# Moving ScalarE's small work away from two slots, and one projection onto earlier slots, in a hand-ordered scan loop

## The chip, the cores and the metric

The kernel runs on one core of one Trainium2 chip. The metric is the device time of that core in microseconds (us). Four engines compute: TensorE (PE in the profile), VectorE (DVE), ScalarE (ACT) and GpSimd (POOL). A fifth queue, SyncE (SP), issues most DMAs. Each engine takes its instructions in the order in which the program wrote them, and waits for the others through semaphores.

## The reference

For an input x of 4 images, 512 channels, 64 x 64 positions (4096 tokens per image):

```
x = x + mamba_block(group_norm(x))      # layer 0
x = x + linear_attention(group_norm(x)) # layer 1
# layer 0, for each of 4 groups of 128 channels, with 256 inner channels:
xi, z = split(layer_norm(x) @ in_proj)
xc    = silu(causal_conv4(xi) + conv_b)
dt, B, C = split(xc @ x_proj);  dt = softplus(dt @ dt_proj + dt_b)
h_t = exp(dt_t * A) * h_{t-1} + (dt_t * xc_t) * B_t     # 16 states per inner channel
y_t = sum over states (h_t * C_t) + xc * D
out = (y * silu(z)) @ out_proj + skip * x
# then a layer norm and a 512 x 512 projection
# layer 1: q, k = relu(...), kq = sum over tokens of k q, out = (v kq / norm) @ w_out
```

All of it is in float32.

## The kernel before, in words

**Steps and slots.** The work is cut into 128 steps: 4 images x 8 tiles of 512 tokens x 4 groups of channels (`steps`, in this order). A step has 32 scans of 512 tokens, each over 128 partitions that hold 32 inner channels x 4 states; the loop takes them two at a time, so a step has `SLOTS` = 16 slots and the whole run 2048. In a slot stand, in the program's order:

- `drive(g+2)` on POOL (L655): the input of the scans (`bx`, 128 x 1024), two slots ahead; three buffers.
- two scans on DVE (L673), into `h`; after each, one `decay` on ACT (L647): the exponential `dA` (128 x 512, in PSUM), three scans ahead; three banks.
- between the two scans, `product` of the slot before on DVE (L696): three quarters of `h` times `c_all`, a bank of PSUM that `c_row` filled by a bf16 matmul. There is one such bank. `product` of an odd slot also issues `c_row` of the next pair of slots, and then `fold_states`: four fp32 matmuls that add the pair's states into `y`.
- in odd slots POOL multiplies the last quarter of `h` (L684).
- `after()`: everything else of the slot.

Two slots differ. `AWAY = (3, 10)` are the slots in which ACT changes its function table twice: in slot 3 to softplus and back (L1066, L1068), in slot 10 to silu and back. `BEHIND = (4, 11)` are the slots after them: there `product` of the slot itself comes right after its second scan, beside that of the slot before.

**What `after()` holds.** Work that is fixed to slots: the next step's time products `time_banks` at 2 and its softplus (`time_steps`) at 3; `out_proj` of the step before at 4 and its copy `with_skip` at 6; at 3, 5, 6, 7, 8 and 9 one piece of `front`, which is the generator `inputs` of the step after next; silu at 10. A matmul of 128 x 512 in fp32 counts as one unit in the program's own count (`work["mm"]`). The six pieces of `front` are: two taps of the convolution's first half (2 units), two more, the same for the second half, then the two products of the gate branch (`pz`, 1 unit each). A result is taken from PSUM by ACT one slot later, through `later(1, ...)`.

**Queues.** Then three queues of generators are asked for a piece each: `ahead` (the next tile's norms), `late` (the second layer norm and projection of the tile before) and `rest` (the attention of the image before). A piece of `late` or `rest` that needs TensorE is taken while `credit` lasts: 3.5 units a slot, less what the slot issued, and at most 2.6 saved. `limit` says how many of the three shared banks (`ps_w`) the queues may hold: 1 in slots 1 to 5, otherwise 2. A generator that yields "free" is asked again without credit. DVE's broad passes over 128 x 2048 (L390, L410) are "wide" and go into slots 3 and 10.

The order that results is fixed when the program is built.

Of the kernel before, what the change touches and what calls it, by code (L numbers as in the profile page):

```python
# [17 lines left out]
NTAP = 4  # L18
# [6 lines left out]
def kernel(  # L25
# [24 lines left out]
    nc = tc.nc  # L50
# [4 lines left out]
    NH = DI // P  # L55
# [21 lines left out]
    held, now, due = [0], [None], []  # L77

    def work_bank(name, behind=1):
        held[0] += behind  # L80
        return ps_w.tile([P, T], F32, tag="w", name=name)

    def free(n=1):
        held[0] -= n

    def later(n, what):

        done = []

        def both():  # L90
            what()
            done.append(True)

        if now[0] is None:
            both()
        else:
            due.append((now[0] + n, both))
        return done

    def soon():  # L100
# [3 lines left out]
    def until(*done):  # L104
        while not all(done):
            yield "wait"
# [4 lines left out]
    def room(when="wait"):  # L111

        while now[0] is not None and held[0] >= limit[0]:
            yield when

    limit, norming = [0], []
# [4 lines left out]
    def mm(out_, lhsT, rhs, abreast=1, **how):  # L121

        work["mm"] += (0.25 if rhs.dtype == BF16 else 1.0) * rhs.shape[-1] / T / abreast
        nc.tensor.matmul(out_, lhsT, rhs, **how)  # L124
# [188 lines left out]
    def aggregate(stats, name):  # L313

        mv = small.tile([P, NC, 2], F32, tag="mv", name=f"mv_{name}", bufs=4)
        for c in range(NC):
            nc.vector.bn_aggr(mv[:, c, :], stats[:, c, :, :].rearrange("p t s -> p (t s)"))
        return mv
# [37 lines left out]
    def bc(v, n):  # L356
        return v.unsqueeze(1).to_broadcast([P, n, v.shape[-1]])

    def layer_norm(v, name, gained):


        def means(parts, what, when):
            yield from room()
            sums = work_bank(f"{what}_sums_{name}")
            for c in range(NC):
                mm(
                    sums[c * LANE : (c + 1) * LANE, :], ones.to_broadcast([P, LANE]), parts[c],
                    start=True, stop=True, abreast=NC,
                )
            got = wk.tile([P, T], F32, tag="sq", name=f"{what}_got_{name}", bufs=4)  # L370

            def take():
                nc.scalar.copy(got, sums)
                free()

            copied = later(1, take)
            yield
            yield from until(copied)
            yield when
            yield from room(when)  # L380
            bank = work_bank(f"{what}_{name}")
            mm(bank, mean.to_broadcast([P, P]), got, start=True, stop=True)
            return bank

        while norming:
            yield "wait"
        norming.append(name)
        mu = yield from means([v[:, c, :] for c in range(NC)], "mu", "one ahead")
        yield "wide"
        nc.vector.tensor_tensor(v, v, bc(mu, NC), ALU.subtract)  # L390
        free()
        yield "free"
        sqs = []
        for c in range(NC):
            sqs.append(wk.tile([P, T], F32, tag="sq", name=f"sq_{name}_{c}", bufs=4))
            nc.scalar.activation(sqs[c], v[:, c, :], AF.Square)
            if c == 1:
                yield "free"
        var = yield from means(sqs, "var", "two ahead")
        rs = wk.tile([P, T], F32, tag="sq", name=f"rs_{name}", bufs=4)  # L400

        def root():
            nc.scalar.activation(rs, var, AF.Ln, bias=eps)
            nc.scalar.activation(var, rs, AF.Exp, scale=-0.5)

        rooted = later(1, root)
        yield
        yield from until(rooted)
        yield "wide"
        nc.vector.tensor_tensor(v, v, bc(var, NC), ALU.mult)  # L410
        free()
        norming.clear()
        yield
        if gained:
            for c in range(NC):
                nc.scalar.activation(
                    v[:, c, :], v[:, c, :], AF.Identity,
                    bias=b_sb[:, c : c + 1], scale=g_sb[:, c : c + 1],
                )
                if c % 2:  # L420
                    yield "free"
# [57 lines left out]
    def shifted(f, xt, t, nm):  # L479
        if t == 0:  # L480
            for o in range(NC):
                nc.vector.bn_stats(f["first"][:, o, 0, :], xt[:, o, :])
                if o % 2:
                    yield
            f["mv"] = aggregate(f["first"], f"first_{nm}")
            f["off"] = small.tile([P, NC], F32, tag="moff", name=f"moff_{nm}")
            nc.vector.tensor_scalar(f["off"], f["mv"][:, :, 0], -1.0, None, ALU.mult)
            nc.vector.memset(f["sum"][:, :, 0:1], 0.0)
            nc.vector.tensor_scalar(f["square"][:, :, 0], f["mv"][:, :, 1], float(T), None, ALU.mult)
            return  # L490
        for o in range(NC):
            for v, func in (("sum", AF.Identity), ("square", AF.Square)):
                unused = wk.tile([P, T], F32, tag="res", name=f"{v}_{nm}_{o}", bufs=2)
                nc.scalar.activation(
                    unused, xt[:, o, :], func, bias=f["off"][:, o : o + 1],
                    accum_out=f[v][:, o, t : t + 1],
                )
            yield "free"
# [13 lines left out]
    def inputs(f, xn, c, nm):  # L512

        xz = f["xz"] = wk.tile([P, 2, NH, T], F32, tag="xz", name=f"xz_{nm}", bufs=3)
        pc = [None] * NH

        def taps(e, ks):
            for k in ks:
                mm(
                    pc[e], w_cv[:, k, e * P : (e + 1) * P], xn[:, c, k : k + T],  # L520
                    start=(k == 0), stop=(k == NTAP - 1),
                )

        def take(e):
            nc.scalar.activation(xz[:, 0, e, :], pc[e], AF.Identity, bias=cb[:, e : e + 1])

        for e in range(NH):
            pc[e] = work_bank(f"pc_{nm}_{e}", 0)
            taps(e, range(NTAP // 2))
            yield  # L530
            taps(e, range(NTAP // 2, NTAP))
            later(1, lambda e=e: take(e))
            yield
        for e in range(NH):
            pz = work_bank(f"pz_{nm}_{e}", 0)
            mm(
                pz, w_z[:, e * P : (e + 1) * P], xn[:, c, NTAP - 1 : NTAP - 1 + T],
                start=True, stop=True,
            )

            later(1, lambda e=e, pz=pz: nc.scalar.copy(xz[:, 1, e, :], pz))
            yield

    def time_banks(f, nm):
# [62 lines left out]
    SLOTS = NH * NQ * JJ  # L607
    AWAY = (3, 10)
# [42 lines left out]
    def drive(g):  # L651
# [5 lines left out]
        )  # L657

    def slot(g, last, after):
        n, e, q, jj = place(g)  # L660
        b, t, c = steps[n]
# [68 lines left out]
    def with_skip(f, xn, c):  # L730
        nc.scalar.copy(xn[:, c, NTAP - 1 : NTAP - 1 + T], f["po"])
# [257 lines left out]
    ahead, late, rest, light = [], [], [], []  # L989

    def add_to(queue, pieces):
        queue.append([pieces, None])
# [40 lines left out]
    with tc.manual_schedule():  # L1033
        credit, seen, mix, held[0], held_x[0] = 0.0, work["mm"], iter(()), 0, 0
        for n, (b, t, c) in enumerate(steps):
            f, nm = fs[n], names[n]
            before = fs[n - 1] if n else None
# [8 lines left out]
            for s in range(SLOTS):  # L1046
                def after():
# [17 lines left out]
                    if s == 3 and nxt is not None:  # L1065
                        nc.scalar.preload_act_table_set("softplus")  # L1066
                        time_steps(nxt, names[n + 1])
                        nc.scalar.preload_act_table_set("natural_log_exp_and_others")  # L1068
                    if s == 6 and before is not None:
                        pb_, pt_, pc_ = steps[n - 1]  # L1070
                        with_skip(before, xn[pb_, pt_], pc_)
                        if pc_ == NC - 1:
                            add_to(late, leave(pb_, pt_))
                    if s in (3, 5, 6, 7, 8, 9):
                        next(front, None)
                    if s == 4 and nxt is not None:
                        to_rows(nxt, 0, names[n + 1])
# [1 line left out]
                    if s == 4 and before is not None:  # L1079
                        pb_, pt_, pc_ = steps[n - 1]  # L1080
# [16 lines left out]
                    ):  # L1097
                        one(light)

                    limit[0] = 1 if 0 < s < 6 else 2  # L1100
                    credit = min(credit + 3.5 - (work["mm"] - seen), 2.6)
                    busy = False
                    for queue in (ahead, late, rest):
                        kind = queue[0][1] if queue else None
                        if queue is ahead or kind == "free" or credit > 0 or kind == "more" and not busy:
                            start = work["mm"]
                            one(queue, ANYWHERE if queue is ahead and (c, s) > (1, 4) else may)
                            credit -= work["mm"] - start
                            busy = busy or work["mm"] - start > 1
# [68 lines left out]
```

## Time and profile before

| | |
|---|---|
| Time before, median of 3 | 8091.57 us (8079.1 to 8095.19) |
| The profiled execution: its own time | 8087.92 us |
| its span, first to last instruction | 8086.2 us |
| before the first scan | 120 us |
| the 2048 slots | 7492 us |
| after the last slot (attention of the last image) | 474 us |
| DVE busy | 7113.0 us (88%) |
| POOL busy | 6890.3 us (85%) |
| PE busy | 6471.4 us (80%) |
| ACT busy | 5514.5 us (68%) |
| TensorE clock granted, mean | 0.888 |

A share of the span is an average over everything; where the time of a slot goes is read from the idle time of DVE in that slot, and from what ended it. To say so by slot, the trace is cut at the start of each slot's first scan. The clock is the share of full speed that TensorE was granted.

### The profile page before, as it was taken

What the parts mean: (1) busy time and instruction counts of PE and PEld (TensorE: products, weight loads), DVE (VectorE), ACT (ScalarE), POOL (GpSimd) and SP (SyncE); (2) the same over time, 40 slices, a digit from 0 to 9 for tenths busy, and PEclk for the clock granted to TensorE, in tenths of its full rate; (3) what the DMA queues carried; (4) which work ended last, traced back from release to release, by engine and by line L of the source; (5) the groups of instructions that cost most, each with busy time, mean ns of one, the idle gap of its engine ahead of it and who ended that gap; (6) DMA issues with size and microseconds to landing.
All of it is one profiled execution on the core that took longest, in us unless ns stands there. A gap on an engine that the chain in (4) does not pass through costs nothing.

```text
span 8086.2 us, 92449 instructions
## 1 busy us (share of the span) xinstructions
PE 6471.4 (80%) x24800; PEld 2115.5 (26%) x24800; DVE 7113.0 (88%) x6815; ACT 5514.5 (68%) x8289; POOL 6890.3 (85%) x4597
## 2 busy tenths in 40 slices
PE   5677777667788878888788888888788888888599
PEld 1111111112222222322222222332222222322144
DVE  5999999999999999899999999999999999998600
ACT  4667777777767777677776767667777777776421
POOL 4999999999989989899998989888999999889600
PEclk8787888788899989898899999899889999999699
DMA  5666666666666666676666666667666666676402
GB/s 160 166 166 160 156 147 153 157 157 166 167 167 156 162 153 156 168 188 176 169 155 164 166 165 155 155 171 187 163 158 160 156 157 152 150 194 176 110 32 89
DMA packets 829199, 1265.98 MB, mean 157 GB/s; under 512 B 183912, under 2 KB 317560, under 8 KB 816384
## 3 DMA queue, kind: packets, MB, share of 16 engines
q1 hardware_dynamic: 804736, 1222.32, 59.7%
q0 software_dynamic: 16896, 33.56, 2.4%
q10 hardware_dynamic: 7040, 4.20, 0.2%
q8 instruction: 194, 3.18, 0.2%
q14 instruction: 333, 2.73, 0.1%
HBM read 1052.78 MB, written 206.57 MB: 156 GB/s over the span
## 4 chain that ended last, share of the span: by engine, by line
DVE 22%; PE 19%; DMA 17%; POOL 14%; issue 10%; ACT 9%; SPq 8%; POOLq 0%; DVEq 0%; ACTq 0%
DVE h L673 14%; POOL bx L655 10%; DMA d_all<-d_rows 9%; DVE h L696 7%; PE pq L124 5%; SPq L622 5%; DMA b_all<-b_rows 4%; ACT dA L647 3%; PE pc L124 3%; PE pr L124 3%; SPq L572 3%; PE y L124 3%; POOL h L684 2%; PE pp L124 1%; DMA c_sb<-c_rows 1%
## 5 line engine op out<-in xcount | busy, mean ns | idle before, releaser
L655 POOL TENSOR_TENSOR bx<-d_all,b_all 128x1024 f32<-128x1024 f32 x2048 | 4817.4, 2371 | 66.9 <-DVE h L673 51.5
L673 DVE TENSOR_TENSOR_SCAN h<-dA,st,bx 128x512 f32<-128x512 f32 x3584 | 4420.5, 1267 | 80.6 <-ACT dA L647 75.4
L647 ACT ACTIVATE dA<-d_all,a_t 128x512 f32<-128x512 f32 x4096 | 2780.4, 688 | 1764.2 <-DVE h L673 1727.5
L696 DVE TENSOR_TENSOR h<-h,c_all 128x768 f32<-128x768 f32 x2048 | 1906.7, 931 | 307.5 <-PE c_all L124 298.2
L124 PE MATMUL y<-h,fold 128*32 128x512 f32 x8192 | 1280.6, 701 | 160.5 <-POOL h L684 156.1
L684 POOL TENSOR_TENSOR h<-h,c_sb 128x512 f32<-128x512 f32 x1024 | 1299.3, 1269 | 121.4 <-DMA c_sb<-c_rows 33.5
L124 PE MATMUL pc<-xn,w_cv 128*128 128x512 f32 x2048 | 1078.8, 662 | 178.2 <-DVE xn L410 116.7
L124 PE MATMUL c_all<-parts,sel 128*128 128x384 bf16 x1024 | 368.3, 360 | 1058.5 <-DVE h L696 1056.1
L124 PE MATMUL pq<-w_qk,xa 128*128 128x512 f32 x2048 | 990.7, 615 | 1.9 <-ACT xa L348 1.9
L673 DVE TENSOR_TENSOR_SCAN h<-dA,bx 128x512 f32<-128x512 f32 x512 | 601.2, 1206 | 58.8 <-ACT dA L647 54.6
L124 PEld LDWEIGHTS pc<-xn,w_cv 128*128 128x128 f32 x2048 | 395.9, 204 | 807.7 <-issue 445.6
L124 PEld LDWEIGHTS <-sel 128*128 128x128 bf16 x1280 | 127.5, 100 | 1724.4 <-DVE h L696 1495.6
L683 POOL COPY st<-h 128x4 f32<-128x4 f32 x1024 | 206.9, 202 | 425.2 <-DVE h L673 382.2
L124 PEld LDWEIGHTS pq<-w_qk,xa 128*128 128x128 f32 x2048 | 402.8, 199 | 468.7 <-issue 446.2
L124 PE MATMUL pr<-xb,m 128*128 128x512 f32 x1024 | 500.4, 626 | 24.8 <-DMA xb<-x 16.5
L124 PE MATMUL pp<-xn,w_pr 128*128 128x512 f32 x1024 | 487.6, 602 | 3.8 <-DVE xn L410 3.8
L124 PEld LDWEIGHTS y<-h,fold 128*32 128x32 f32 x8192 | 170.9, 114 | 743.6 <-issue 281.0
L124 PE MATMUL y<-xz,dg 32*32 32x512 f32 x2048 | 340.4, 741 | 0.0
L720 POOL TENSOR_TENSOR xz<-xz 128x512 f32<-128x512 f32 x256 | 325.4, 1271 | 2.7 <-ACT xz L717 2.7
L561 POOL TENSOR_TENSOR dt<-dt,xz 128x1024 f32<-128x1024 f32 x128 | 302.2, 2361 | 25.5 <-ACT dt L553 25.5
L124 PE MATMUL pd<-xz,w_xp 128*128 128x512 f32 x512 | 311.6, 740 | 7.8 <-ACT xz L987 7.8
L771 ACT ACTIVATE kq<-pq 128x512 f32<-128x512 f32 x256 | 150.6, 588 | 232.6 <-PE pq L124 230.5
(169 smaller groups left out, 6063.9 us busy)
## 6 DMA issues: line engine op xcount, KB each, us to landing
d_all<-d_rows SPq DMA_DIRECT2D x2048, 256.0 KB, 6.6
b_all<-b_rows SPq DMA_DIRECT2D x4096, 64.0 KB, 2.2
d_rows<-dt SPq DMA_DIRECT2D x256, 512.0 KB, 3.7
c_sb<-c_rows SPq DMA_DIRECT2D x4096, 16.0 KB, 1.9
xs<-in_x_dram SPq DMA_DIRECT2D x32, 1024.0 KB, 5.8
xn<-in_x_dram SPq DMA_DIRECT2D x32, 1024.0 KB, 5.7
xr<-in_x_dram POOLq DMA_DIRECT2D x32, 1024.0 KB, 11.2
x<-xr SPq DMA_DIRECT2D x32, 1024.0 KB, 4.3
```

The lines of the kernel that those rows point to most:

```text
L124: nc.tensor.matmul(out_, lhsT, rhs, **how)
L561: nc.gpsimd.tensor_tensor(f["both"][:, 1], f["both"][:, 0], f["xz"][:, 0], ALU.mult)
L572: nc.sync.dma_start(d[k * BLK : (k + 1) * BLK, v], src)
L622: nc.sync.dma_start(dst[k * BLK : (k + 1) * BLK, :], rows_[q * KS + k, :].partition_broadcast(BLK))
L647: nc.scalar.activation(dAs[k], fs[n]["d_all", e][:, 0, j, :], AF.Exp, scale=a_t[:, e, j, q : q + 1])
L655: nc.gpsimd.tensor_tensor(bxs[g], fs[n]["d_all", e][:, 1, jj * 2 : jj * 2 + 2, :], bc(b_all[g // JJ], 2), ALU.mult)
L673: nc.vector.tensor_tensor_scan(h[:, j, :], dAs.pop(2 * g + i), bxs[g][:, i, :], 0.0 if t == 0 else st[:, c, e, q, j : j + 1], ALU.mult, AL ...
L683: nc.gpsimd.tensor_copy(st[:, c, e, q, :], h[:, :, T - 1])
L684: nc.gpsimd.tensor_tensor(h[:, :, CUT:], h[:, :, CUT:], bc(c_sb.pop(g // JJ), NJ), ALU.mult)
L696: nc.vector.tensor_tensor(own, own, bc(c_all[g // JJ], 2), ALU.mult)
L720: nc.gpsimd.tensor_tensor(f["xz"][:, 1, e, :], f["xz"][:, 1, e, :], f["xz"][:, 0, e, :], ALU.mult)
L771: nc.scalar.activation(qk[i], pq, AF.Relu)
```

## The change

1. `later`: what falls due in slot 3 or 10 is done in the slot after.
2. In those two slots a piece of `late` or `rest` that yielded "free" (work of ACT, mostly) is not taken. Two `yield`s of those generators now say "free": in `layer_norm` before the gain, and in `shifted` ahead of its eight ACT passes.
3. `front` has four pieces instead of six, at slots 5, 6, 7 and 8: the two products of the gate branch stand beside the two pieces of the convolution's first half (3, 3, 2 and 2 units).
4. `with_skip` (and the start of `leave`) moves from slot 6 to slot 5.
5. `limit` is 0 in slot 3, 1 in slots 1, 2, 4, 5 and 6, otherwise 2.

```diff
-            due.append((now[0] + n, both))
+            at = now[0] + n
+            due.append((at + 1 if at % SLOTS in AWAY else at, both))
...
         norming.clear()
-        yield
+        yield "free"
         if gained:
...
             return
+        yield "free"
         for o in range(NC):
             for v, func in (("sum", AF.Identity), ("square", AF.Square)):
...
-        for e in range(NH):
-            pc[e] = work_bank(f"pc_{nm}_{e}", 0)
-            taps(e, range(NTAP // 2))
-            yield
-            taps(e, range(NTAP // 2, NTAP))
-            later(1, lambda e=e: take(e))
-            yield
-        for e in range(NH):
+        def gate_branch(e):
             pz = work_bank(f"pz_{nm}_{e}", 0)
             mm(
                 pz, w_z[:, e * P : (e + 1) * P], xn[:, c, NTAP - 1 : NTAP - 1 + T],
                 start=True, stop=True,
             )
-
-            later(1, lambda e=e, pz=pz: nc.scalar.copy(xz[:, 1, e, :], pz))
+            later(1, lambda: nc.scalar.copy(xz[:, 1, e, :], pz))
+
+        for e in range(NH):
+            pc[e] = work_bank(f"pc_{nm}_{e}", 0)
+            taps(e, range(NTAP // 2))
+            if e == 0:
+                gate_branch(0)
+            yield
+            taps(e, range(NTAP // 2, NTAP))
+            later(1, lambda e=e: take(e))
+            if e == 0:
+                gate_branch(1)
             yield
...
-                    if s == 6 and before is not None:
+                    if s == 5 and before is not None:
...
-                    if s in (3, 5, 6, 7, 8, 9):
+                    if s in (5, 6, 7, 8):
                         next(front, None)
...
-                    limit[0] = 1 if 0 < s < 6 else 2
+                    limit[0] = 0 if s == 3 else 1 if s in (1, 2, 4, 5, 6) else 2
...
                         kind = queue[0][1] if queue else None
+                        if kind == "free" and s in AWAY and queue is not ahead:
+                            continue
```

## The prediction

> **What bounds the kernel now.** First the page: no engine is full, DVE comes nearest.
>
> ```profile
> PE 6471.4 (80%) x24800; PEld 2115.5 (26%) x24800; DVE 7113.0 (88%) x6815; ACT 5514.5 (68%) x8289; POOL 6890.3 (85%) x4597
> ...
> L673 DVE TENSOR_TENSOR_SCAN h<-dA,st,bx 128x512 f32<-128x512 f32 x3584 | 4420.5, 1267 | 80.6 <-ACT dA L647 75.4
> ...
> L696 DVE TENSOR_TENSOR h<-h,c_all 128x768 f32<-128x768 f32 x2048 | 1906.7, 931 | 307.5 <-PE c_all L124 298.2
> ```
>
> The last column is DVE's idle time ahead of the group. Where nothing waits, a slot lasts 3.22 us (two scans, one product). The step's mean is 58.6 us over the 126 middle steps; DVE idles 3.48 of them (438 us in all). By slot: 1.71 in slot 4, 0.50 in slot 12, 0.47 in slot 7, 0.28 in slot 5, under 0.17 elsewhere. So the question is who ends DVE's waits in these four slots. The waits of DVE, longest first:
>
> ```profile
> DVE h L696 <- PE c_all L124: 298.2, 165, 6.0
> DVE kq L778 <- PE pk L124: 242.4, 42, 7.6
> DVE h L673 <- ACT dA L647: 130.1, 64, 46.7
> ```
>
> The second is the attention of the last image, after the slots, and is not touched. The first is 207 us in slot 4 and 52 in slot 7; the third is 62 in slot 12, 18 in slot 5, and start-up. A timeline of slots 3 and 4 of step 90 shows how slot 4 comes to wait (start, length, engine, line):
>
> ```profile
> 5382.49 2.08 PE L124 MATMUL pt<-dt,w_dt 32*128 32x512 f32 x4
> 5385.96 3.78 PE L124 MATMUL pc<-xn,w_cv 128*128 128x512 f32 x4 [1.39 <-DVE xn L410]
> 5389.53 2.57 PE L124 MATMUL pr<-xb,m 128*128 128x512 f32 x4
> 5391.94 0.33 PE L124 MATMUL c_all<-parts,sel 128*128 128x384 bf16 x1
> ```
>
> and DVE at the same time:
>
> ```profile
> 5387.86 1.27 DVE L673 TENSOR_TENSOR_SCAN h<-dA,st,bx 128x512 f32<-128x512 f32 x1
> 5392.30 0.95 DVE L696 TENSOR_TENSOR h<-h,c_all 128x768 f32<-128x768 f32 x1 [3.17 <-PE c_all L124]
> ```
>
> In slot 4 the row of C is asked for one scan (1.2 us) before its use, and it stands behind slot 3's work: a piece of the convolution that waited for a bank (here until DVE's wide pass had read it), then `pr`. And the four `pc` matmuls took 3.78 us, against 2.57 for four of `pr` half of which ran at full speed. The windows of this step say why (last but two: clock):
>
> ```profile
> 5377.20:5380.40 3.20, 1.40 (x10) 0.25 (x9) 3.20 (x4) 2.42 (x5) 2.96 (x4) 1.00 0.90 191
> 5380.40:5385.80 5.40, 4.17 (x16) 0.70 (x12) 5.40 (x5) 3.40 (x5) 5.32 (x4) 0.53 1.05 212
> 5385.80:5393.20 7.40, 7.24 (x19) 2.64 (x19) 4.23 (x6) 3.90 (x5) 7.37 (x4) 0.65 0.69 166
> 5393.20:5395.50 2.30, 2.30 (x15) 0.82 (x12) 2.30 (x3) 0.69 (x1) 0.00 (x0) 1.00 0.47 179
> ```
>
> PE was quiet in slot 2 (1.40 us busy), and ran slots 3 and 4 at 0.53 and 0.65 of its clock. Over all steps the clock is 0.76, 0.76, 0.79, 0.83 in slots 1 to 4 and 0.97 to 0.99 in 5 to 9.
>
> **What the Trainium skill says, and whether this trace agrees.** (1) The Trainium skill, *TensorE: Matmul & The Clock Gate*, section "Part 1: The HAM clock gate": after one idle window of about 3.4 us TensorE runs at half clock, and about one busy window brings it back. The trace agrees: its clock records are 0.5 or 1.0 and multiples of 3.413 us long. Of 167 such windows at full clock with PE under 40% busy none was followed by a fast one; of those over 50% nearly all; of 261 half-clock windows over 90% busy, 88%. (2) The same page, section "Step-by-step: what each phase is for": matmuls stay in program order. Agrees: `c_all` ran after `pr`. (3) *ScalarE: Activation LUTs*, section "What ACT_TABLE_LOAD costs": 1283 ns, plus a drain of 1380. The trace has 1283 ns and the next activation 0.02 us later: no drain, and I use 1.28.
>
> **The change, part by part** (per step; 126 steps count).
>
> *Slot 4.* In the changed program's order the work that PE gets in slot 3's `after()` falls from 3.0 to 0.3 units. Nothing then stands ahead of the row of C. 1.68 us (what this product waits) become about 0.1: **-1.58**.
>
> *Slots 5 to 7.* The 2.7 units go to slots 5 and 6. Between the row for slot 4 and the row for slot 6 PE now has 9.35 units instead of 7.89 (quarter points 8, 9.5, 11; before 6, 8, 9.25). Time there: from the end of slot 4's first product to the product of slot 7 are 8.9 us without waits, so that row must start 8.4 us after the first one. In before, a full-clock stretch with 10 units took 9.4 us: 0.36 for the row and about 0.88 a unit. For 7, 8, 9.5 and 11 units (shares 0.2, 0.2, 0.25, 0.35) that is 6.5, 7.4, 8.7 and 10.0 us: late by 0, 0, 0.3 and 1.6, mean 0.64. At half clock more. After slot 2's work (about 3.5 us) PE has nothing until the row of slot 4: 3 us where slot 3 has no wide pass, over 5 where it has (2.26 us more, 67 of 126 steps). That makes an idle window in my estimate in 85% of the steps. The burst then starts at half clock and stays there for the rest of that window and one full one, 3.4 to 6.8 us, mean 4.8: 2.4 us of work lost. Late then by 0.5, 1.4, 2.7, 4.0, mean 2.46. 0.85 x 2.46 + 0.15 x 0.64 = 2.19, against 0.41 now: **+1.78**. The next row (slot 9's product) has 6.7 units instead of 6.1 and PE no lead: 8 units in a quarter of the steps are 1 us late: 0.38 against 0.09, **+0.29**.
>
> *ACT at the table changes.* In slot 12 DVE waits for `dA` in the 40 steps whose slot 10 has no DVE extra, 1.47 us each. Two loads, silu (1.91) and a `dA` (0.69) are 5.2 us behind the one before; the DVE work in that time leaves 0.7 us. The gate's copy (0.58) and the `shifted` passes (0.14 of each kind, about 0.9 a pair) account for the rest, and leave: 40 x 0.77 and small ones, **-34 us** over the run. Slot 5's 18 us go to a third: **-12**. The order shows slot 3 not free of other work: the next tile's `group_norm` (L348, half an activation a step) stays.
>
> *Where it goes.* The moved copies stand in slots 4 to 9. ACT idles 16.4 us a step, and a `dA` is 2 us early there or more; nothing on DVE waits. `with_skip`, a slot earlier, may wait for `po` on ACT with two `dA` behind it; those have the same lead. POOL's instructions and SP's DMAs keep their slots (a store of the attention may go one later). POOL is 2.7 to 6 us ahead of the scans in slots 5 to 8, so it does not become the bound for a gain of 1.6. The tail holds 475.1 units either way. A little more attention falls into slots 13 to 1: **+8**.
>
> Sum: 126 x (1.78 + 0.29 - 1.58) = +62; -34 - 12 + 8 = -38; **+24 us** on the profiled execution's 8087.9, so **8112 us**. The median shown stands 3.7 above that execution, inside the spread of 16.
>
> **The rivals.** *A, the forecast:* the wait moves from slot 4 to slot 7 and grows, since PE goes cold in the emptied slot 3. *B, on the other side:* PE stays warm. With share p of cold starts the sum is 126 x (0.64 + 1.82 p - 0.41 + 0.29 - 1.58) - 38; at p = 0 that makes 7916, at 0.5 8031; it turns at 0.75. For it: slot 3's own stalls on banks are gone, and PE that was cold in slot 2 works longer and may be warm by then. Against: the counts above. *C:* the two cancel, within 0.2%. *D:* A, and PE's lateness reaches ACT, which waits in order for `po`, `pz`, `pc` and `y` in slots 5 to 9 with the `dA` behind: 0.6 us more a step, 8190. Against: ACT waits 1.0 us a step for these now (xz L717 99.9 us, xz L525 22.2, the others 4.4), and it shows nowhere on DVE. *E, the edit does less than it says:* `group_norm` in slot 3 keeps some of slot 5's wait; worth at most 12 us.
>
> **How the numbers follow.** 0.2% (16 us) is about what a measurement of this kernel can tell from no change. A 0.44 and D 0.12 are slower: 0.56; C 0.12; B 0.32. The predicted time is A's, 8112, whose own range is 8100 to 8170. B reaches down to 7916, and lies at 8031 where half of the steps are warm; I take 7985 below and D's 8190 above.
>
> **What would show it.** Right: DVE's wait for `c_all` nearly gone in slot 4 and 2 us in slot 7; clock at slots 4 and 5 below 0.8; slot 12's wait for `dA` halved. Wrong: clock over 0.85 in slots 4 to 5 and slot 7's wait under 1 us (B), or `dA` waits on DVE in slots 6 to 10 (D).

## The result, and the profile after

The changed kernel is slower: 8215.80 us (median of 4 runs, 8211.47 to 8218.85) against 8089.92 (8079.10 to 8095.19), a ratio of 1.0158 [1.0145, 1.0171]. Its profiled execution took 8218.36 us (span 8216.4), 130 us more than that of the kernel before. The forecast, 8112, had the side right and the size wrong; its range ended at 8190.

The page of the changed kernel, busy time and costliest groups (last column: idle time of the engine just before the group, and what ended most of it):

```profile
PE 6489.0 (79%) x24800; PEld 2118.6 (26%) x24800; DVE 7121.6 (87%) x6815; ACT 5516.5 (67%) x8289; POOL 6886.4 (84%) x4597
...
L678 DVE TENSOR_TENSOR_SCAN h<-dA,st,bx 128x512 f32<-128x512 f32 x3584 | 4433.2, 1271 | 109.1 <-ACT dA L652 54.4
...
L701 DVE TENSOR_TENSOR h<-h,c_all 128x768 f32<-128x768 f32 x2048 | 1916.2, 936 | 383.6 <-PE c_all L125 365.5
```

DVE is busy for only 8.6 us more than before, so nearly all of the loss is waiting. The waits of DVE, us in total, times, longest:

```profile
DVE h L701 <- PE c_all L125: 365.5, 179, 8.6
DVE kq L783 <- PE pk L125: 251.4, 46, 7.6
DVE h L678 <- ACT dA L652: 109.7, 71, 48.5
DVE h L678 <- POOL bx L660: 56.1, 45, 5.7
```

The wait for `c_all` grew by 67 us and that for `dA` fell by 20. The last line was 6.8 us before: here is a wait that the prediction said would not come. "The row" of a slot is, in what follows, the bank `c_all` that its product reads; one row serves two slots, so the rows that matter are those for slots 4, 6 and 8, and a late one shows as a wait in slot 4, 7 or 9. Cut by slot over the 126 middle steps (DVE's idle time, us):

| | before | after | change | forecast |
|---|---|---|---|---|
| `c_all`, slot 4 | 208 | 3 | -205 | -199 |
| `c_all`, slot 7 | 52 | 258 | +206 | +224 |
| `c_all`, slot 9 | 11 | 45 | +34 | +37 |
| `dA`, slots 12 and 5 | 81 | 56 | -25 | -46 |
| `bx` of POOL | 6 | 55 | +49 | 0 |
| `c_all`, slot 15 | 18 | 52 | +34 | } +8 |
| attention and statistics | 40 | 59 | +20 | |
| other `c_all` and `dA`; gaps under 150 ns | 23 | 32 | +9 | 0 |
| all of DVE's idle time | 438 | 561 | +123 | +24 |

With the 8 us by which DVE is busier in these steps, that is the whole 130. The attention after the last slot takes the same time in both (474 and 473 us). The first three rows come to +35 against a forecast of +62; the loss that was missed is below them.

First the part that was right. PE in slots 4 to 7 of step 90 of the changed kernel (start, length, line, operation; the last bracket is the idle time before):

```profile
5481.70 0.50 PE L125 MATMUL c_all<-parts,sel 128*128 128x384 bf16 x1 [3.66 <-DVE h L701]
5482.13 1.94 PE L125 MATMUL y<-h,fold 128*32 128x512 f32 x8
5484.00 1.93 PE L125 MATMUL po<-xn,skd 32*32 32x512 f32 x8
5485.86 2.47 PE L125 MATMUL po<-xz,w_op 128*128 128x512 f32 x4
5488.17 1.88 PE L125 MATMUL pp<-xn,w_pr 128*128 128x512 f32 x4
5489.89 1.88 PE L125 MATMUL pc<-xn,w_cv 128*128 128x512 f32 x4
5491.60 1.02 PE L125 MATMUL pz<-xn,w_z 128*128 128x512 f32 x2
5492.46 1.88 PE L125 MATMUL pp<-xn,w_pr 128*128 128x512 f32 x4
5494.18 0.33 PE L125 MATMUL c_all<-parts,sel 128*128 128x384 bf16 x1
5494.43 1.07 PE L125 MATMUL y<-h,fold 128*32 128x512 f32 x8
```

DVE, at the product that needs the second row:

```profile
5488.20 2.45 DVE L678 TENSOR_TENSOR_SCAN h<-dA,st,bx 128x512 f32<-128x512 f32 x2
5494.54 0.95 DVE L701 TENSOR_TENSOR h<-h,c_all 128x768 f32<-128x768 f32 x1 [3.89 <-PE c_all L125]
```

The row for slot 4 now leaves as soon as DVE has freed its bank: nothing stands ahead of it, and PE had been idle for 3.66 us. Then slot 4's own work (`y`, `po`) and the moved work come in one block of 12 us without a gap, and the row for slot 6 stands behind it. Its first half runs slowly: the eight `y` matmuls take 1.94 us at the block's start and 1.07 at its end. The windows of slots 2 to 6 of this step (after the length: busy time of PE, PEld, DVE, ACT and POOL; then PE's clock, the DMA share and GB/s):

```profile
5470.90:5474.10 3.20, 1.03 (x5) 0.29 (x9) 3.20 (x4) 2.42 (x5) 2.96 (x4) 0.86 1.06 212
5474.10:5479.50 5.40, 3.94 (x20) 0.50 (x12) 5.40 (x5) 3.39 (x5) 5.32 (x4) 0.77 1.07 214
5479.50:5483.80 4.30, 2.10 (x9) 0.31 (x9) 4.20 (x5) 3.90 (x5) 4.30 (x3) 0.56 0.57 150
5483.80:5486.20 2.40, 2.40 (x13) 0.54 (x10) 2.40 (x4) 0.69 (x1) 2.40 (x2) 0.50 0.42 114
5486.20:5489.40 3.20, 3.20 (x7) 1.30 (x7) 3.20 (x5) 1.72 (x3) 3.12 (x4) 0.90 0.72 285
```

The clock is 0.56 and 0.50 in slots 4 and 5; in the kernel before the cold slots of this step were 3 and 4. Over all steps the clock in slots 4 and 5 is 0.70 and 0.70 (before 0.83 and 0.99), and 76% of the steps have over 1 us at half clock between the two rows. The forecast had 85%.

### The profile page after: what moved, and what is told of

Same layout as the page of the kernel before. It is cut to its first block, busy times and chain, and to the rows that moved or that the text cites. A ratio compares the mean times of both kernels' runs of the same rounds, so it can differ in the third digit from the quotient of the medians.

```text
span 8216.4 us, 92462 instructions
## 1 busy us (share of the span) xinstructions
PE 6489.0 (79%) x24800; PEld 2118.6 (26%) x24800; DVE 7121.6 (87%) x6815; ACT 5516.5 (67%) x8289; POOL 6886.4 (84%) x4597
## 4 chain that ended last, share of the span: by engine, by line
PE 23%; DVE 21%; DMA 18%; POOL 12%; issue 10%; SPq 8%; ACT 6%; POOLq 0%; DVEq 0%; ACTq 0%
DVE h L678 13%; DMA d_all<-d_rows 10%; POOL bx L660 8%; DVE h L701 6%; PE pq L125 4%; SPq L627 4%; PE y L125 4%; PE pc L125 3%; PE po L125 3%; DMA b_all<-b_rows 3%; SPq L577 3%; ACT dA L652 3%; PE pr L125 2%; POOL h L689 2%; PE pp L125 2%
## 5 line engine op out<-in xcount | busy, mean ns | idle before, releaser
L125 PE MATMUL y<-h,fold 128*32 128x512 f32 x8192 | 1334.4, 729 | 194.9 <-POOL h L689 190.0
L125 PE MATMUL pc<-xn,w_cv 128*128 128x512 f32 x2048 | 1014.0, 618 | 5.3 <-ACT xn L417 4.6
L125 PEld LDWEIGHTS pc<-xn,w_cv 128*128 128x128 f32 x2048 | 369.4, 192 | 615.7 <-issue 580.8
L125 PE MATMUL po<-xz,w_op 128*128 128x512 f32 x512 | 293.6, 700 | 2.0 <-POOL xz L725 2.0
```

## The experiments

Unless said otherwise the diff is against the changed kernel, and the ratio against the kernel before on the same chip (8086.8 to 8088.0 us).

### Which part costs

`act_only`: parts 1 and 2 alone; the changed kernel without the new `front`, `with_skip` and `limit`.

```diff
-                    if s == 5 and before is not None:
+                    if s == 6 and before is not None:
...
-                    if s in (5, 6, 7, 8):
+                    if s in (3, 5, 6, 7, 8, 9):
...
-                    limit[0] = 0 if s == 3 else 1 if s in (1, 2, 4, 5, 6) else 2
+                    limit[0] = 1 if 0 < s < 6 else 2
```

> Parts 1 and 2 of the change alone, on the kernel before (what falls due in slots 3 and 10 a slot later, 'free' pieces not taken there); the gate's second copy stays in slot 10, since silu needs it. Theory A (the loss is TensorE's: its work is crowded into slots 4 to 6 after an empty slot 3): these parts are no loss; DVE's wait for dA in slot 12 falls from 62 us to 30 to 45, nothing else moves: 8050 to 8085 against 8090. Rival R1 (ACT's moved work is late where it went, in slots 4 to 9, and holds back POOL and DVE): a large part of the +126 us shows here: 8130 or more.

`pe_side`: parts 3, 4 and 5 alone.

```diff
-            due.append((at + 1 if at % SLOTS in AWAY else at, both))
+            due.append((now[0] + n, both))
...
-        yield "free"
+        yield
...
-                        if kind == "free" and s in AWAY and queue is not ahead:
-                            continue
```

> Parts 3, 4 and 5 alone (four front pieces at slots 5 to 8, with_skip at 5, the limits), without parts 1 and 2. A: the whole loss is here, 8210 to 8250; DVE waits about 2 us a step for c_all in slot 7, at a clock of 0.7 in slots 4 and 5. R1: less than half of it, under 8150.

`act_only` took 8071.73 us, 0.9980 [0.9973, 0.9987]; `pe_side` 8240.56, 1.0189 [1.0172, 1.0206]. What relieves ACT gains 15 us (slot 12's wait for `dA` falls from 62 to 51, less than the 30 to 45 expected); what moves PE's work costs 154, more than the whole change, as A expected. The waits of DVE in `pe_side`:

```profile
DVE h L699 <- PE c_all L124: 377.3, 188, 11.4
...
DVE h L676 <- POOL bx L658: 45.3, 43, 5.4
```

The `c_all` waits come with parts 3 to 5, and so do most of those for POOL. But `act_only` has some of these too, 20 us where the kernel before had 7:

```profile
DVE h L675 <- POOL bx L657: 20.1, 33, 2.3
```

### Cold clock or too much work between the two rows

The forecast let both act: 9.35 units instead of 7.89, and half clock. `after_warm` keeps PE busy in slot 3 with matmuls by a zero operand: six, and more after a wide pass.

```diff
+                    if s == 3:
+                        for _ in range(6 + round(3.5 * extra[0])):
+                            nc.tensor.matmul(
+                                ys[n, 0], minus[0 : 2 * LANE, :], bqk[0 : 2 * LANE, :],
+                                start=False, stop=False, skip_group_check=True,
+                            )
```

> The changed kernel, with matmuls of zeros added to y at the end of slot 3 (64 rows of bf16 zeros, 512 columns; 6 of them, and 3.5 for each us of DVE's additional work in that slot), which change no value and wait for nothing: TensorE does not stand idle in slot 3. A1 (of the 2.05 us wait in slot 7 most is half clock): clock in slots 4 and 5 rises from 0.70 to 0.9 or more, slot 7's wait falls to 0.6 to 1.0 us, 8215 to 8040 - 8090. A2 (it is the 9.35 units of work, or banks, at whatever clock): the wait stays over 1.6 us and the time is 8180 or more; the zeros themselves may even delay the row of slot 4.

8184.12 us, 1.0121 [1.0106, 1.0136]: a miss for A1; A2 had the time and the delayed row, but not the wait. Slots 4 and 5 have a clock of 0.84 and 0.83, and slot 7's wait falls only from 258 to 177 us (1.4 a step, where A2 expected over 1.6); and the zeros stood ahead of the row of slot 4, whose wait is 85 us again.

`after_thin45` takes work out instead: no queue piece that needs a bank in slots 4 and 5.

```diff
-                    limit[0] = 0 if s == 3 else 1 if s in (1, 2, 4, 5, 6) else 2
+                    limit[0] = 0 if s in (3, 4, 5) else 1 if s in (1, 2, 6) else 2
```

> The changed kernel with limit 0 in slots 4 and 5 as well: the queues open no bank there, so TensorE has 7.0 units (in every step) between the rows for slots 4 and 6, not 9.35, and 8.5 instead of 6.7 between the rows for slots 6 and 8. A1 (half clock costs 2.4 us in most steps): slot 7 still waits 0.4 to 0.8 us and slot 9 about 1: 8100 to 8150. A2 (work alone): with 7 units nothing waits in slot 7, slot 9 0.3 us: about 8000.

8146.53 us, 1.0071 [1.0055, 1.0086], inside the range of A1; its waits were split otherwise. Slot 7's falls to 40 us (0.31 a step, expected 0.4 to 0.8) with the clock at 0.72 and 0.70, but the work comes back ahead of slot 9, whose wait rises from 45 to 185 (1.5 a step, expected 1).

`after_front3` starts `front` in slot 3 again, in pieces of 2, 3, 3 and 2 units.

```diff
-            if e == 0:
-                gate_branch(0)
+            if e == 1:
+                gate_branch(1)
...
             if e == 0:
-                gate_branch(1)
+                gate_branch(0)
...
-                    if s in (5, 6, 7, 8):
+                    if s in (3, 5, 6, 7):
```

> The changed kernel with the first front piece (2 units) back in slot 3 and the gate's products one piece later: pieces of 2, 3, 3 and 2 units at slots 3, 5, 6 and 7. Between the rows for slots 4 and 6 TensorE still has 9.2 units (9.35 in the changed kernel), but slot 3 is not empty. A1 (half clock): clock in slots 4 and 5 over 0.85, slot 7's wait falls from 2.05 us to under 1.0, slot 4's comes back to 0.4 to 0.9: 8110 to 8170. A2 (only the number of units counts): slot 7 still waits 1.8 us or more, and slot 4 0.5: 8230 or more.

8193.66 us, 1.0132 [1.0116, 1.0149], outside what either theory expected. The clock is back at 0.80 and 0.97, yet slot 7 still waits 155 us, and slot 4 waits 131 again. The means (9.2 units, 1.2 us a step) hide two kinds of steps. In 39 of the 126 PE still has over 1 us at half clock between the two rows, and these hold 95 of the 155 us. At full clock 7 or 8 units wait 0.03 us a step (53 steps), and about 11 units 2.0 (25 steps): what does not fit at full clock is the steps with most work.

`after_front3_thin` is the opposite case: pieces of 2, 3, 2 and 3 at slots 5 to 8, no queue piece with a bank in 3, 4 and 5, so that 6.0 units lie between the rows and PE stays cold.

```diff
-            if e == 0:
-                gate_branch(0)
...
-            if e == 0:
-                gate_branch(1)
+            gate_branch(e)
...
+                    limit[0] = 0 if s in (3, 4, 5) else 1 if s in (1, 2, 6, 7) else 2
```

> As after_2332_gap, but limit 0 in slots 3, 4 and 5 and 1 in slots 1, 2, 6 and 7: 6.0 units between the rows for slots 4 and 6 in every step, and 8.5 before the next. A: slot 7 waits under 0.1 us although the clock in slots 4 and 5 is 0.7, slot 9 1.0 to 1.4 us: 8040 to 8100. Rival (the cold clock alone brings slot 7's wait, whatever the work): slot 7 waits over 0.5 us.

8086.98 us, 1.0002 [0.9993, 1.0010]. The clock is 0.71 and 0.68, as cold as in the changed kernel, and slot 7's waits for `c_all` are 2.3 us in all. **A cold start alone makes no wait: 6 units fit even so.** The queue work returns before slot 9 (177 us). All of DVE's waits for `c_all`:

```profile
DVE h L698 <- PE c_all L125: 226.9, 142, 5.1
```

The changed kernel itself shows the two together. Its steps sorted by units between the rows, with slot 7's mean wait: 7 units, 0.60 us where PE had over 1 us at half clock (14 steps) and none otherwise (6); 8 units, 1.37 us at low clock (19) and 0.08 at full clock (10); 9 to 10.2 units, 1.85 (11) and 0.24 (8); above, 3.64 (52) and 1.79 (6). So at full clock up to 9 units nearly fit, and at half clock even 7 are late.

### Other places for the work

`after_front6789`: `front` one slot later, and no bank for the queues in 3, 6 and 7; some of the attention is then left for after the slots, where the time grows from 474 to 488 us.

```diff
-                    if s in (5, 6, 7, 8):
+                    if s in (6, 7, 8, 9):
...
+                    limit[0] = 0 if s in (3, 6, 7) else 1 if s in (1, 2, 4, 5) else 2
```

> The changed kernel with the four front pieces at slots 6, 7, 8 and 9, and limit 0 in slots 3, 6 and 7, otherwise 1 in slots 1 to 5; the convolution's second result is taken in slot 10 ahead of silu. Slot 3 is as empty as in the changed kernel, but between the rows for slots 4 and 6 stand 6.5 units, then 7.1, then 8.0. The attention is not finished in the slots: 32 units more come after them, about +28 us. Theory A: half clock in slots 4 and 5 as before (0.7), yet slot 7 waits under 0.4 us, since 6.5 units cold fit the 8.4 us; slots 9 and 11 wait 0.3 to 0.6 each: 8050 to 8110 with the tail. Rival (what counts is that slot 3 is empty, wherever the work goes): 8200 or more.

8079.73 us, 0.9990 [0.9984, 0.9997], in the range of theory A: slot 7's wait is 54 us (0.43 a step, where under 0.4 was expected), with slot 3 still empty and the clock at 0.68 and 0.71 in slots 4 and 5. What is new is 70 us in slot 11.

`act_lim3`: `act_only`, with no bank for the queues in slot 3 (`limit[0] = 0 if s == 3 else 1 if 0 < s < 6 else 2`).

> Parts 1 and 2 (as in act_only) and of part 5 limit 0 in slot 3 alone; the front pieces and with_skip stay where the kernel before has them. TensorE's work from slot 3 falls from 3.0 to 2.0 units and does not become empty. Theory A (an emptied slot 3 and a crowd in slots 4 to 6 are the loss; less in slot 3 is good): DVE's wait for c_all in slot 4 falls from 1.66 us to about 0.8 (steps of the kernel before with 2 units there waited 0.46), slot 7's rises by 0.1 to 0.3: 7960 to 8040. Rival (what leaves slot 3 only comes back as a wait in slot 7): 8060 or more.

8062.09 us, 0.9964 [0.9951, 0.9977]: the rival's side, at its edge. Slot 4's wait falls from 209 to 130 us only: the first piece of the convolution is still in slot 3. Of the 79 us gained there 58 come back as waits in slots 7 and 9 (against `act_only`).

`after_2332_gap`: pieces of 2, 3, 2 and 3 at 5 to 8, and no bank for the queues in 3, 4 and 6.

```diff
+            gate_branch(e)
...
+                    limit[0] = 0 if s in (3, 4, 6) else 1 if s in (1, 2, 5, 7) else 2
```

> The changed kernel with the same four slots for front, but each gate product beside a second half (pieces of 2, 3, 2 and 3 units at slots 5 to 8), and limit 0 in slots 3, 4 and 6, 1 in slots 1, 2, 5 and 7. Between the rows of C for slots 4 and 6 stand 7.2 units (at most 8.25; the changed kernel 9.35, up to 11.25), then 7.4 and 6.3; the attention is finished in the slots. Theory A (a cold start of 2.4 us in three steps of four, and 0.88 us a unit): slot 4 waits 0, slot 7 0.4 to 0.6 us, slot 9 0.3 to 0.6; with bx, slot 15 and attention as in the changed kernel 7990 to 8060, ahead of both. Rival (the wait only moves on, to slot 9 or 11): 8100 or more.

8066.56 us, 0.9976 [0.9966, 0.9987]; a little above the expected range. Slot 7 waits 58 us, as expected, and slot 9 83 (0.66 a step, expected 0.3 to 0.6).

`spread_3678`: one piece early, three late, and a gap for the queues ahead of slot 9's row.

```diff
+            gate_branch(e)
...
-                    if s in (5, 6, 7, 8):
+                    if s in (3, 6, 7, 8):
...
-                    limit[0] = 0 if s == 3 else 1 if s in (1, 2, 4, 5, 6) else 2
+                    limit[0] = 0 if s in (3, 7) else 1 if s in (1, 2, 4, 5, 6) else 2
```

> The changed kernel with front pieces of 2, 3, 2 and 3 units at slots 3, 6, 7 and 8 (each gate product beside a second half) and limit 0 in slots 3 and 7. Slot 3 keeps 2 units, so TensorE is not empty there; 5.9, 6.1, 6.4 and 6.9 units stand before the rows of C for slots 4, 6, 8 and 10 (in the changed kernel 3.9, 9.4, 6.7 and 5.2). Theory A (what a row waits for is the units between it and the last row, plus half clock after a quiet slot): DVE waits 100 to 140 us for c_all in slot 4 as in the other kernels with 2 units in slot 3, under 30 us each in slots 7, 9 and 11; clock in slot 5 over 0.95; bx near 20: 7985 to 8030, the fastest of all. Rival (each move only sends the wait on): 8060 or more.

**8030.08 us, 0.9926 [0.9913, 0.9940]: faster than both kernels**, at the upper end of what was expected. Its clock in slots 4 and 5 is 0.80 and 0.97. Slot 4 keeps 139 us, slot 7 has 13, slot 9 35, slot 11 28; `bx` is 33, where 20 was expected. Its waits of DVE:

```profile
DVE h L698 <- PE c_all L125: 253.0, 197, 6.1
...
DVE h L675 <- ACT dA L649: 80.8, 38, 46.0
DVE h L675 <- POOL bx L657: 33.2, 34, 3.7
```

Against the changed kernel 112 us of `c_all` and 29 of `dA` are gone, and 23 of `bx`.

### Why POOL became late

In the changed kernel the `bx` waits lie in slots 8 (38 us) and 7 (11). Two edits move work of POOL. `after_pad` takes away a wait of POOL, for the norm that it copies from (34 us of POOL's idle time in slot 7):

```diff
         yield from layer_norm(body, f"a_{b}_{t}", True)
+        yield from pause(1)
         nc.gpsimd.tensor_copy(pad, xn[:, :, T : T + NTAP - 1])
```

> The changed kernel with the copy of the tile's last columns on POOL (pad, once in four steps) one slot later. In the changed kernel POOL waits for ACT there (pad behind xn L417, 33.6 us in slot 7, which in turn stand behind with_skip waiting for po), and DVE's waits for bx are 55 us against 6. P1 (POOL is late because it waits for ACT there): bx waits fall to under 25 us, 8185 to 8200. P2 (POOL is late because its slots 3 to 7 are full and DVE now comes earlier): bx waits stay over 40 us, 8205 to 8225.

`after_dt6` moves one product of POOL (2.35 us) from slot 4 to slot 6:

```diff
                         to_rows(nxt, 0, names[n + 1])
+                    if s == 6 and nxt is not None:
                         to_rows(nxt, 1, names[n + 1])
```

> The changed kernel with one POOL instruction, the multiply of 128 x 1024 in to_rows (2.36 us) and its store, two slots later (slot 6 instead of 4). P2 (DVE's new waits for bx, 55 us, come from POOL being full in slots 3 to 7 while DVE reaches slots 5 to 8 earlier): bx waits fall under 25 us if the multiply then falls behind bx of slot 8, 8170 to 8200. P3 (POOL is late for another reason, or there is no room in slots 6 to 8 either, since DVE waits in slot 7 and POOL has been brought forward): bx waits stay over 45 us, 8205 or more.

`after_pad`: 8213.17 us, 1.0158 [1.0142, 1.0173], `bx` waits 55 us: that wait of POOL was not the cause, and P2 stands, that POOL is full there while DVE comes earlier. `after_dt6`: 8228.85 us, 1.0174 [1.0159, 1.0189], `bx` waits 66 us, as P3 expected. It did bring POOL's lead at slot 7 (from the end of `bx` to the scan that reads it) from 1.83 to 3.69 us, and slot 7 waits no more; but slot 8 still waits 36 us, and slot 9, behind the moved product, now 18.

The trace shows what the long waits have in common. Step 76 of the changed kernel has one of the longest waits; its slot 3 begins at 4609.6 and slot 8 at 4633.1. SP's issues, POOL and then DVE:

```profile
4617.75 0.30 SPq L627 DMA_DIRECT2D b_all<-b_rows  x1
4620.85 7.11 SPq L627 DMA_DIRECT2D c_sb<-c_rows  x4
```

```profile
4611.60 1.27 POOL L466 DMA_DIRECT2D xr<-in_x_dram  x1
...
4623.76 0.18 POOL L688 COPY st<-h 128x4 f32<-128x4 f32 x1
4629.54 1.26 POOL L689 TENSOR_TENSOR h<-h,c_sb 128x512 f32<-128x512 f32 x1 [5.59 <-DMA c_sb<-c_rows]
4630.76 4.67 POOL L660 TENSOR_TENSOR bx<-d_all,b_all 128x1024 f32<-128x1024 f32 x2
```

```profile
4633.15 1.28 DVE L678 TENSOR_TENSOR_SCAN h<-dA,st,bx 128x512 f32<-128x512 f32 x1 [5.70 <-POOL bx L660]
```

The four small loads of the last quarter of C took 7.11 us to issue. For this pair of slots the mean is 4.1 us (3.9 in the kernel before), for six of the eight pairs 1.8 to 2.0. Each of the last three was released by the end of a `d_all` transfer of 256 KB. POOL's product of the last quarter waited for them, and the next two `bx` stood behind it. The DMA engines were full then (share, the last column but one, over 1 from slot 3 through slot 6; it counts the time of all packets that start in the window, so it can pass 1):

```profile
4609.60:4613.90 4.30, 4.30 (x22) 1.50 (x19) 4.30 (x6) 2.80 (x5) 4.30 (x3) 1.00 1.08 295
4613.90:4618.20 4.30, 3.57 (x18) 0.90 (x20) 4.20 (x5) 4.26 (x5) 4.22 (x5) 1.00 1.08 223
4618.20:4620.80 2.60, 2.60 (x13) 1.06 (x6) 2.51 (x3) 2.60 (x6) 2.60 (x2) 1.00 1.10 259
4620.80:4624.00 3.20, 2.59 (x10) 0.83 (x12) 3.20 (x4) 3.20 (x6) 3.14 (x3) 1.00 1.11 264
```

What is unusual there is the 1 MB accumulation of `xr` (L466), the end of a piece of `late`, issued in slot 3 of this step. In the 11 steps with `xr` in slot 3 the share in slots 4, 5 and 6 is 1.09, 1.13 and 1.02, of which `xr`'s own queue is 0.39, 0.90 and 0.47; in the steps without a large transfer in slot 3 or 4 the share is 0.76, 0.52 and 0.65. Before, all `xr` of the middle steps but one were issued between slot 14 and slot 1; in the changed kernel 11 fall into slot 3. Of its 126 middle steps 14 have a 1 MB transfer issued in slot 3 or 4, and these hold 33 of the 49 us of `bx` waits in slots 7 and 8: 2.4 us a step, against 0.14 in the others. Six of the 14 hold 29 of the 33; in each of them the load of the next tile (`xn`) had gone out in slot 2 or 3, and a second transfer of 1 MB (four times `xr`, twice `xb`) followed in slot 3 or 4. The other seven steps with `xr` in slot 3 hold 4.4 us. Of the 48 us of `bx` waits over 0.5 us anywhere in the step, 40 follow within three slots on a wait of POOL for a transfer.

No run changes `xr`'s slot alone, so this link is read from the trace, and the other traces say that it is not the whole cause. `after_front6789` issues no `xr` in slot 3 or 4 and still waits for `bx`:

```profile
DVE h L678 <- POOL bx L660: 37.8, 40, 3.4
```

`after_front3` and `spread_3678` have none there either (30 and 33 us), and in `after_thin45` the steps with a 1 MB transfer in slot 3 or 4 hold 6 of 44 us. The kernel before has seven steps with such a transfer, and not one waits. What goes with these waits across the kernels is slot 4. The eight kernels in which DVE waits 4 us or less for `c_all` there have 37 to 66 us of `bx` waits; the five that keep about 130 us or more there have 6 to 33; `after_warm`, with 85, has 47. While DVE waited in slot 4, POOL got ahead: its lead at slot 5 was 6.08 us before and is 4.25 in the changed kernel, while at slot 4 it hardly differs (2.44 and 2.31).

## Why the prediction was wrong in size

**Right.** Slot 4's wait goes (1.68 to 0.13 us a step); it returns in slot 7 (0.41 to 2.05, forecast 2.19); slot 9's grows (0.09 to 0.36, forecast 0.38). The three rows make +35 us against +62. The clock behaved as said, and the forecast's signs on PE came. Rival B's condition, a warm start, did not arise. Rival D's path, PE's lateness reaching DVE through ACT, did not show: ACT did wait more for `po` and `pz` (76.0 and 102.9 us in all), yet `dA` waits fell. That the kernel came out slower is partly luck for the forecast: the three rows and `dA` together are +10 us (35 less 25), within what it calls no change. Nearly all the rest of the 130 us are waits that it had put at 0 or 8.

**The step that failed** is "POOL is 2.7 to 6 us ahead of the scans in slots 5 to 8, so it does not become the bound for a gain of 1.6", and with it "POOL's instructions and SP's DMAs keep their slots". It cost 49 us where nothing was written.

The first of the two takes means for the whole. Before, POOL's lead at slot 7 was 3.40 us on average, but 1.0 or less in a tenth of the steps, and at slot 8 0.45. DVE now spends 1.55 us less a step in slot 4, and POOL's lead at slot 7 is 1.83 us (0.03 in a tenth of the steps). Without a large transfer in slot 3 or 4 it is 2.00, so most of the fall is not the transfers'. An estimate: 1.55 us taken from each lead at slot 7 of the kernel before leaves 17 us of waits there; 11 were measured.

The second holds for what is fixed to a slot. The queues' pieces carry transfers of 1 MB, and parts 3 to 5 change when a piece is taken: `xr` went from slots 14 to 1 into slots 1 and 3, and the steps with a large transfer in slot 3 or 4 hold 33 us of `bx` waits. How the two share the loss was not tried, and stays open.

**The term of +8 for more attention** was mis-sized: it is +54 (slot 15, attention and statistics). The attention of each of the first three images ends 28 slots later, by its last store. Of the 34 us in slot 15, 24 are three events, in steps 63, 95 and 123, in which `pr` sits on PE waiting 8 to 9 us for the 1 MB load of its tile, and a row stands behind it. Why that load is late was not tried.

**The ACT term** was -46 and is -25: slot 12 gives 27 of the 34, slot 5 nothing (18 to 20 us). `act_only` shows slot 5 at 7 us, so the relief is there, and is used up when the matmul side moves too; which wait does it was not followed.

**The weights of clock and work** were nearly right. The forecast had slot 7 wait 0.64 us a step after a warm start and 2.46 after a cold one. The changed kernel's own steps give 0.88 and 2.36 for the same mix of work (an estimate: the means by class given above, each weighted by all the steps of its amount of work). Together with `after_front3_thin` they show that both count: 6 units fit even at half clock, 7 begin to be late there, and at full clock the limit lies near 9.

## What to carry to other kernels

Before emptying a slot, count what must fit between the next two fixed deadlines at the clock that the gap leaves; work that is moved out of one deadline's way is in the next one's. And when a queue of background work is throttled in one place, list the large transfers that its pieces issue and see in which slots they land: the steps with a 1 MB transfer in slot 3 or 4 hold 33 us of waits, as much as the three rows of the matmul moves together (35), though what part the transfer itself has in them is open. A lead is to be counted by its low end, not by its mean: a gain of 1.6 us was set against a mean lead of 3.40, and a tenth of the steps had 1.0. `spread_3678` kept the good half of the change by leaving one piece in the slot and giving each later deadline a gap of its own.

## What had not been expected of the hardware

- Keeping PE busy by a few zero matmuls raised the clock in slots 4 and 5 only from 0.70 to 0.84 and 0.83, and slot 4's wait rose from 3 to 85 us, where the zeros stand ahead of a wanted row.
- Four DMA issues of 16 KB took 7.11 us of the SP queue while the DMA share was above 1, where this pair of slots takes 4.1 on average, though the loads themselves land in 1.8 us (median): the last three were each released by the end of a transfer of 256 KB.
